# A fused two-layer graph network: the fold of two attention units one product earlier, the range check behind the keys, the last store in two halves

## The chip, the core and the metric

The kernel runs on one core of one Trainium2 chip. Five engines work side by side: TensorE (PE) multiplies matrices, with its weight loads shown as a row of their own (PEld); VectorE (DVE) and ScalarE (ACT) do elementwise work and reductions; GpSimd (POOL) does a little elementwise work; SyncE (SP) issues nearly all DMAs. The metric is the device time of one execution in microseconds (us). Three runs of the kernel before give 2157.03 to 2157.29, median 2157.13.

## What is computed

Sixteen batch elements x of 1024 nodes and 256 channels pass through two layers; adj is a 1024 by 1024 matrix, the same for all. All is in float32.

```python
# layer 0
c_adj = mean of x over channels                      # one number a node
A     = abs(abs(sigmoid(c_adj[j] - c_adj[i]) - 0.5) - 0.5) * 2
Wg    = adj * (A + A.T) / 2
g     = relu((x.T @ Wg) * para)                      # 256 x 1024
q     = g.T in 4 heads of 64;  k, v = x @ kv_w in 4 heads
out   = softmax(q @ k.T * scale) @ v
x     = layernorm(x + out)
# layer 1: two graph convolutions, 256 -> 128 -> 256
h = relu(x @ w1_loop + adj @ (x @ w1_neigh) + b1)
h = relu(h @ w2_loop + adj @ (h @ w2_neigh) + b2)
x = layernorm(x + (x + h) * 0.5)
```

## The kernel before

The kernel sets its order of work by hand: each engine runs its instructions in the order in which `run()` (from line 973, it calls all parts) writes them down. One pass of its loop treats one batch element b: attention of b, in between the graph convolutions of b - 1 and b - 2 and the last normalisation of b - 3, and then the queries, keys and values of b + 1.

**Attention.** The work of one b is cut into four units (`UNITS`: two pairs of heads by two halves of the query nodes). `scores(u)` makes eight score tiles on PE, takes their exponential on ACT (L629) and sums them on DVE over the key tiles (L633, L635); a transpose and a reduction (L637, L640) leave partial denominators in `den_part`. `outputs(u)` multiplies with the values on PE (L648) and transposes the result on DVE (L653). `add(*units)` is the fold of the change's name. A small matmul with the constant `fold` sums the partial denominators over partitions (L662). DVE takes the reciprocal (L668), and for each unit scales the output, adds it to x and takes channel sums (L672, L674, L675). After the last unit the two halves of the sums are joined (L256), and `rden_min` and `rden_max` note the extremes of the reciprocals for this b (L678, L679). These two feed nothing but the check at the very end: if a reciprocal left a given range, a slow, safe version of everything is run.

**Queries.** For b + 1 the product x.T @ Wg is made with seven block products in place of eight (`FastQueries`), on four steps k of 128 rows. `likeness` makes A on ACT, `times_adj` multiplies by adj on DVE (L496), `right` makes the sums of blocks T that the seven products need (L549 to L552, four instructions of DVE), and `pair(k)` does both for step k. `step(k)` issues the seven products on PE (L577), in the order 1, 2, 3, 5, 7, 6, 4, and in the last step 1, 6, 2, 7, 4, 5, 3. Products 5 and 6 read T. A function can be handed to a step (`halfway`); it is called ahead of product 7. The lines of `run()` that concern the change, for every b from 1 to 14:

```python
q.pair(2)
q.step(0)
q.step(1, lambda: att.add(*((2, 3) if both else (3,))))
q.pair(3)
q.step(2, norm.mean)
q.load_para()
kv.load()
q.step(3)
qT = q.end(norm.sum_squares, norm.squares)
```

So DVE's queue reads: products with adj and T of pair 2, the fold of units 2 and 3, products with adj and T of pair 3, the mean. PE's reads: steps 0 and 1 with the small matmul inside, steps 2 and 3. In the first pass of this kind (b = 1) unit 2 has been folded before, and step 1 folds unit 3 alone.

**Keys and values.** `kv.run` interleaves seven products each for keys and values on PE with copies on ACT and additions on DVE; the last addition is L461. In its midst the variance is folded, and POOL takes the power -0.5 (L328). Behind it `norm.scale` multiplies x by that (L333), and `norm.spread` transposes it (L221) and stores it by nodes (eight DMAs, L341).

**The end.** For the last b, `ending` treats the output in quarters of two node tiles. The first three are normalised on ACT, the last on DVE (`normalize`, L289), and each is stored with one DMA (L876). Behind the last store SP loads the result of the range check into a register and branches on it (L1213, L1214).

Buffers: 25 row tiles of 128 by 1024 are handed out in turn (`row_tile`), and PSUM (the memory that PE writes) has three tiles of two banks and two of one bank.

Of the kernel before, what the change touches and what calls it, by code (L numbers as in the profile page):

```python
# [18 lines left out]
def kernel(  # L19
# [266 lines left out]
    def normalize(mv, rstd, xb, count=NT):  # L286

        for t in range(count):
            nc.vector.tensor_scalar(xb[:, t, :], xb[:, t, :], mv[:, t, 0:1], rstd[:, t:t + 1],  # L289
                                    op0=ALU.subtract, op1=ALU.mult)  # L290
# [223 lines left out]
    class FastQueries(Queries):  # L514
# [42 lines left out]
            self.times_adj(TJ + k)  # L557
            self.right(k)

        def step(self, k, halfway=None):  # L560
            if k == 0:
                a, b, c = (big_psum(f"g_ps_{self.b}_{i}") for i in range(3))
                h0, h1 = ts(0, FB), ts(1, FB)
                self.p = {1: a[:, h0], 6: a[:, h1], 2: b[:, h0], 7: b[:, h1], 5: c[:, h0], 3: c[:, h1],
                          4: bank_psum(f"g_ps_{self.b}_3")}
            lo, hi = self.wg.pop(k), self.wg.pop(TJ + k)
            t12, t4 = self.T.pop(k)
            h0, h1 = ts(0, FB), ts(1, FB)
            terms = {1: (self.block(0, 0), lo[:, h0]), 2: (self.block(0, 1), hi[:, h0]), 3: (self.S[3], hi[:, h1]),
                     4: (self.block(1, 1), t4), 5: (self.S[0], t12[:, h0]), 6: (self.S[1], t12[:, h1]),  # L570
                     7: (self.S[2], lo[:, h1])}

            for n in (1, 6, 2, 7, 4, 5, 3) if k == TJ - 1 else (1, 2, 3, 5, 7, 6, 4):
                if n == 7 and halfway:
                    halfway()
                x_n, w_n = terms[n]
                nc.tensor.matmul(self.p[n], x_n[:, k, :], w_n, start=(k == 0), stop=(k == TJ - 1))  # L577
# [26 lines left out]
    class Attention:  # L604
# [50 lines left out]
        def add(self, *units):  # L655

            b, half = self.b, FB // S
            u0, n = units[0], len(units)
            pd = bank_psum(f"den_ps_{b}_{u0}")
            den = pd[:, 0:2 * half * n]  # L660
            part = [self.parts.pop(u) for u in units][0]
            nc.tensor.matmul(den, fold.rearrange("p a k -> p (a k)"),  # L662
                             part[:, u0 % 2:u0 % 2 + n, :].rearrange("p u k -> p (u k)"), start=True, stop=True)
            den = den.rearrange("p (u s h) -> p u s h", u=n, s=2)
            rden = self.rden[:, u0 * half:(u0 + n) * half].rearrange("p (u h) -> p u h", u=n)
            for s in range(2):
                rows = slice(s * HD, (s + 1) * HD)
                nc.vector.reciprocal(rden[rows], den[rows, :, s, :])  # L668
            for k, u in enumerate(units):
                pair, j = UNITS[u]  # L670
                o = by_node(self.o.pop(u))
                nc.vector.tensor_mul(o, o, rden[:, k, :].unsqueeze(2).to_broadcast([P, half, S]))  # L672
                dst = by_node(self.xB[pair][:, ts(j, FB)])
                nc.vector.tensor_add(dst, dst, o)  # L674
                nc.vector.tensor_reduce(self.sums[:, pair, ts(j, half)], dst, AX.X, ALU.add)  # L675
            if u == len(UNITS) - 1:
                join(self.sums)
                nc.vector.tensor_reduce(rden_min[:, b:b + 1], self.rden, AX.X, ALU.min)  # L678
                nc.vector.tensor_reduce(rden_max[:, b:b + 1], self.rden, AX.X, ALU.max)  # L679

    def safe_attention(b, xb, qT, kT, v):

# [54 lines left out]
    class GraphConv:  # L737
# [119 lines left out]
        def ending(self, dst, rows01, aside):  # L857

            per = FB // C
            parts, banks = [], {}

            def leave(g, mv, rstd, aside=True):
                rows = self.x[:, g * per:(g + 1) * per, :]
                if aside:
                    shift = small.tile([P, per], F32, tag="shift_e", name=f"shift_e_{g}", bufs=2)
                    nc.vector.tensor_scalar_mul(shift, mv[:, :, 0], -1.0)
                    nc.gpsimd.tensor_mul(shift, shift, rstd)  # L870
                    for i in range(per):
                        nc.scalar.activation(rows[:, i, :], rows[:, i, :], AF.Identity, bias=shift[:, i:i + 1],
                                             scale=rstd[:, i:i + 1])
                else:
                    normalize(mv, rstd, rows, per)
                nc.sync.dma_start(out=dst[g * per * P:(g + 1) * per * P, :].rearrange("(t p) c -> p t c", p=P), in_=rows)  # L876

            def bias(g):
                banks[g] = (bank_psum if g % 2 else half_psum)(f"h2e_ps_{g}")
                nc.scalar.copy(banks[g].rearrange("p (i c) -> p i c", c=C),  # L880
                               b2_sb.unsqueeze(1).to_broadcast([P, per, C]))

            def quarter(g):
                p2 = banks.pop(g)
                self.outer(g, per, p2, onto=True)
                rows = self.x[:, g * per:(g + 1) * per, :]
                nc.vector.scalar_tensor_tensor(rows, p2.rearrange("p (i c) -> p i c", c=C), 0.0, rows,
                                               op0=ALU.max, op1=ALU.add)
                mv = small.tile([P, per, 2], F32, tag="mv_e", name=f"mv_e_{g}", bufs=2)
                statistics(mv, rows, range(per), f"e{g}")  # L890
                rstd = reciprocal_deviation(mv, f"e{g}", EPS2, per)
                parts.append((g, mv, rstd))

            self.second(rows01, lambda: (bias(0), bias(1), aside(), bias(2), bias(3), quarter(0)))
            leave(*parts.pop())
            for g in range(1, NT // per):
                quarter(g)
                leave(*parts.pop(), aside=g + 1 < NT // per)
# [74 lines left out]
    def run():  # L973
# [57 lines left out]
        for b in range(B):  # L1031
# [85 lines left out]
            if more and not c1:  # L1117
                kv = KeysValues(b + 1, ready["xT"])
                for t in range(3, NT):
                    q.load(t)  # L1120
                for t in range(3, NT):
                    q.likeness(t)
                tiles[2] = adj_blocked(2)
                q.times_adj(3)
                q.step(0)
                q.times_adj(4)
                q.step(1)
                att.add(3)
                for mt in (3, 5, 6, 7):
                    tiles[mt] = adj_blocked(mt)  # L1130
                q.load_para()
                q.times_adj(5)
                q.step(2)
                q.step(3)
                norm.mean()
                q.times_adj(6)
                q.times_adj(7)
                q.step(4)
                norm.squares()
                norm.sum_squares()  # L1140
                q.step(5)
                q.step(6)
                kv.sums()
                kv.load()
                norm.variance()
                xB = load_blocked(b + 1, f"a{b + 1}")
                q.step(7)
                qT = q.end()
                load_next()
                kT, v = kv.run(later=lambda: (norm.scale(), norm.spread(), turn_adj((2, 3))))  # L1150
                turn_adj((5, 6, 7))
            elif more:
                q.pair(2)
                q.step(0)
                q.step(1, lambda: att.add(*((2, 3) if both else (3,))))
                q.pair(3)
                q.step(2, norm.mean)
                q.load_para()
# [3 lines that stand above are left out]
                xB = load_blocked(b + 1, f"a{b + 1}")  # L1162
                load_next()
                kT, v = kv.run(norm.variance, q.scale)
                if not c2:
                    adj_sums(rows01, 3)
                norm.scale()
                norm.spread()
            else:
                c2.load_h1()  # L1170
                c2.load_x()
                both.fetch(2, 3)
                c1.inner()
                both.left(nc.gpsimd)
                both.fetch(1, 4)
                both.run({1: (lambda: att.add(3),), 2: (norm.mean, norm.squares, norm.sum_squares), 7: (norm.variance,),
                          5: (norm.scale, norm.spread)})
                c1.turn(0)
                c2.last()
                c1.turn(1)  # L1180
# [86 lines left out]
```

## Time and profile before

| what | value |
|---|---|
| median of 3 runs | 2157.13 us (2157.03 to 2157.29) |
| the profiled execution | 2157.04 us, its span 2155.3 us |
| granted TensorE clock | 0.998 |
| one pass of the loop | about 132.6 us |
| DVE L668, reciprocal on 64 x 32 | 0.35 us, 52 of them |
| DVE L678, minimum over 64 columns | 0.21 us, 16 of them |
| DVE L551 and L552, one T block | 0.68 and 0.69 us |
| POOL L328, power on 128 x 32 | 6.24 us, 16 of them |
| last four stores, issue to landing | 2.1 to 4.4 us, median 3.4 |

The busy time of PE comes from matmuls whose ends are modelled, and its instructions overlap; the time from one start to the next is the surer measure. A wait is put down to the semaphore that came last. A line of the timeline reads: start, duration, engine, line, operation, out<-in, shape, count, and in brackets the idle time before it with what ended it.

### The profile page before, as it was taken

Reading aid. Unit: us, or ns where it says so; the run is one execution under the profiler, and the core shown is the slowest. Engines: PE = TensorE matmul, PEld = TensorE weight load, DVE = VectorE, ACT = ScalarE, POOL = GpSimd, SP = SyncE. Lnnn points to the kernel's source line nnn. Section 1 sums busy time; section 2 is a strip of 40 time slices with the busy share of each in tenths; the row PEclk is TensorE's granted clock in tenths of the full one; section 3 lists DMA queues with packets and bytes.
Section 4 is the critical chain, followed back from the end, with each engine's and each line's share of the span. In section 5 each row is a group of like instructions: output and inputs, shape, how many; then the busy total and the mean of one; then the engine's idle time right before and its main releaser. Section 6 shows DMA issues by size and latency. Waiting matters only on the chain.

```text
span 2155.3 us, 23725 instructions
## 1 busy us (share of the span) xinstructions
PE 2142.7 (99%) x8360; PEld 1021.6 (47%) x8360; DVE 1903.6 (88%) x2350; ACT 1042.7 (48%) x1374; POOL 358.2 (17%) x201
## 2 busy tenths in 40 slices
PE   9999999999999999999999999999999999999997
PEld 5344444544445444444544445454454444544354
DVE  5999988989999899989999898999899898999964
ACT  5745545545345454445544555445553445545412
POOL 1010130211303113030120302203021130211021
PEclk9999999999999999999999999999999999999999
DMA  9393654736557275472756637565374553734442
GB/s 237 117 147 117 148 156 112 152 108 134 144 143 173 86 132 156 132 171 88 123 167 130 157 91 119 172 127 156 110 115 156 128 156 121 133 128 95 120 138 98
DMA packets 612192, 290.73 MB, mean 135 GB/s; under 512 B 504801, under 2 KB 569697, under 8 KB 612065
## 3 DMA queue, kind: packets, MB, share of 16 engines
q1 hardware_dynamic: 611792, 288.87, 55.6%
q8 instruction: 68, 1.11, 0.2%
q14 instruction: 60, 0.48, 0.1%
q10 hardware_dynamic: 272, 0.26, 0.0%
HBM read 242.35 MB, written 46.72 MB: 134 GB/s over the span
## 4 chain that ended last, share of the span: by engine, by line


## 5 line engine op out<-in xcount | busy, mean ns | idle before, releaser
L629 ACT ACTIVATE pr<-s 128x1024 f32<-128x1024 f32 x512 | 476.1, 1054 | 175.8 <-PE s L626 175.0
L635 DVE TENSOR_TENSOR acc<-acc,pr 128x1024 f32<-128x1024 f32 x384 | 489.2, 1274 | 42.2 <-DVE acc L635 2.4
L626 PE MATMUL s<-qT,kT 64*128 64x512 f32 x2048 | 456.8, 596 | 0.0
L648 PE MATMUL av<-pr,v 128*64 128x512 f32 x2048 | 453.6, 595 | 0.0
L626 PEld LDWEIGHTS s<-qT,kT 64*128 64x128 f32 x2048 | 190.9, 186 | 237.3 <-ACT pr L629 116.0
L328 POOL TENSOR_TENSOR rstd<-rstd,neg_half 128x32 f32<-128x32 f32 x16 | 99.8, 6238 | 1118.0 <-DVE rstd L326 1118.0
L648 PEld LDWEIGHTS av<-pr,v 128*64 128x64 f32 x2048 | 141.3, 137 | 298.7 <-issue 292.2
L490 ACT ACTIVATE wg<-c_row,c_col 128x1024 f32<-128x1024 f32 x128 | 146.1, 1141 | 75.6 <-DVE accB L637 65.7
L496 DVE SCALAR_TENSOR_TENSOR wg<-wg,adj 128x1024 f32<-128x1024 f32 x128 | 149.9, 1209 | 12.2 <-ACT wg L491 11.9
L932 PE MATMUL hu_ps<-adj,R 128*128 128x512 f32 x360 | 158.0, 595 | 0.0
L491 ACT ACTIVATE wg<-wg 128x1024 f32<-128x1024 f32 x128 | 135.3, 1057 | 4.1
L577 PE MATMUL g_ps<-wg,S 128*128 128x512 f32 x224 | 116.4, 601 | 0.0
L577 PE MATMUL g_ps<-T,S 128*128 128x512 f32 x224 | 115.7, 598 | 0.0
L577 PE MATMUL g_ps<-wg,x 128*128 128x512 f32 x224 | 109.0, 599 | 0.0
L633 DVE TENSOR_TENSOR acc<-pr,pr 128x1024 f32<-128x1024 f32 x64 | 82.0, 1282 | 29.7 <-ACT pr L629 29.7
L932 PE MATMUL hu_ps<-adjT,t 128*128 128x512 f32 x240 | 105.7, 592 | 0.0
L932 PEld LDWEIGHTS hu_ps<-adj,R 128*128 128x128 f32 x360 | 67.3, 190 | 78.9 <-issue 78.2
L586 ACT COPY P<-g_ps 128x512 f32<-128x512 f32 x14 | 8.2, 585 | 178.2 <-PE g_ps L577 178.2
L637 DVE STREAM_TRANSPOSE accB<-acc 128x1024 f32<-128x1024 f32 x64 | 79.7, 1245 | 2.2
L948 ACT COPY snap<-hu_ps 128x512 f32<-128x512 f32 x15 | 8.8, 585 | 150.2 <-PE hu_ps L932 150.2
L640 DVE TENSOR_REDUCE den_part<-accB 128x32 f32<-128x1024 f32 x64 | 78.1, 1220 | 2.2
L820 PE MATMUL h_ps<-w2n_sb,uT 128*128 128x256 f32 x240 | 72.7, 385 | 0.0
(204 smaller groups left out, 3018.1 us busy)
## 6 DMA issues: line engine op xcount, KB each, us to landing
adj<-in_adj_dram SPq DMA_DIRECT2D x128, 512.0 KB, 4.8
adj<-adjT SPq DMA_DIRECT2D x120, 512.0 KB, 10.1
para<-in_L_gnn_para_dram SPq DMA_DIRECT2D x32, 512.0 KB, 4.5
xB_a<-in_x_dram SPq DMA_DIRECT2D x128, 128.0 KB, 3.9
x1d<-xB_a SPq DMA_DIRECT2D x128, 128.0 KB, 3.4
x<-x1d SPq DMA_DIRECT2D x16, 1024.0 KB, 15.5
xB<-in_x_dram SPq DMA_DIRECT2D x120, 128.0 KB, 4.5
x<-in_x_dram SPq DMA_DIRECT2D x15, 1024.0 KB, 6.9
```

The costliest lines, as they stand in the source:

```text
L328: nc.gpsimd.tensor_tensor(self.rstd, self.rstd, neg_half, ALU.pow)
L490: nc.scalar.activation(wg, self.c_row, AF.Abs, bias=self.c_col[:, t:t + 1], scale=-1.0)
L491: nc.scalar.activation(wg, wg, AF.Tanh, scale=-0.5)
L496: nc.vector.scalar_tensor_tensor(wg, wg, 1.0, self.adj.pop(t), op0=ALU.add, op1=ALU.mult)
L577: nc.tensor.matmul(self.p[n], x_n[:, k, :], w_n, start=(k == 0), stop=(k == TJ - 1))
L626: nc.tensor.matmul(ps[:, ts(s, FB)], self.kT[rows, pair, ts(mt, P)], self.qT[rows, pair, ts(j, FB)], start=True, stop=True)
L629: nc.scalar.activation(pr, ps, AF.Exp)
L633: nc.vector.tensor_add(acc, self.pr[0], pr)
L635: nc.vector.tensor_add(acc, acc, pr)
L637: nc.vector.transpose(accB, acc)
L648: nc.tensor.matmul(pav[s * HD:(s + 1) * HD, :], self.v[:, mt, pair * P + s * HD:pair * P + (s + 1) * HD], self.pr[mt][:, ts(s, FB)], start ...
L932: nc.tensor.matmul(dst, self.x[n][:, k, :], half_adj[w][:, k, :] if w else of_rows(rows, k), start=(start and k == 0), stop=(k == TJ - 1), ...
```

## The change

Three things are done. A step gets a parameter that says ahead of which product the function is called, and step 1 is given 5 in place of 7. The two reductions of the range check leave `add` and become a function `watch`, which is called where `add` was last in the first and the last batch element, and behind `kv.run` in all others. The last quarter of the output is normalised and stored tile by tile.

```diff
-        def step(self, k, halfway=None):
+        def step(self, k, halfway=None, at=7):
...
-                if n == 7 and halfway:
+                if n == at and halfway:
                     halfway()
...
             if u == len(UNITS) - 1:
                 join(self.sums)
-                nc.vector.tensor_reduce(rden_min[:, b:b + 1], self.rden, AX.X, ALU.min)
-                nc.vector.tensor_reduce(rden_max[:, b:b + 1], self.rden, AX.X, ALU.max)
+
+        def watch(self):
+            b = self.b
+            nc.vector.tensor_reduce(rden_min[:, b:b + 1], self.rden, AX.X, ALU.min)
+            nc.vector.tensor_reduce(rden_max[:, b:b + 1], self.rden, AX.X, ALU.max)
...
                     for i in range(per):
                         nc.scalar.activation(rows[:, i, :], rows[:, i, :], AF.Identity, bias=shift[:, i:i + 1],
                                              scale=rstd[:, i:i + 1])
+                    nc.sync.dma_start(out=dst[g * per * P:(g + 1) * per * P, :].rearrange("(t p) c -> p t c", p=P),
+                                      in_=rows)
                 else:
-                    normalize(mv, rstd, rows, per)
-                nc.sync.dma_start(out=dst[g * per * P:(g + 1) * per * P, :].rearrange("(t p) c -> p t c", p=P), in_=rows)
+                    for i in range(per):
+                        normalize(mv[:, i:i + 1, :], rstd[:, i:i + 1], rows[:, i:i + 1, :], 1)
+                        t = g * per + i
+                        nc.sync.dma_start(out=dst[t * P:(t + 1) * P, :], in_=rows[:, i, :])
...
                 att.add(3)
+                att.watch()
...
-                q.step(1, lambda: att.add(*((2, 3) if both else (3,))))
+                q.step(1, lambda: att.add(*((2, 3) if both else (3,))), 5)
...
                 kT, v = kv.run(norm.variance, q.scale)
+                att.watch()
...
-                both.run({1: (lambda: att.add(3),), 2: (norm.mean, norm.squares, norm.sum_squares), 7: (norm.variance,),
+                both.run({1: (lambda: att.add(3), att.watch), 2: (norm.mean, norm.squares, norm.sum_squares), 7: (norm.variance,),
```

## The prediction, made before the changed kernel was run

> **What bounds the kernel now.** I read the page first, then the windows of one pass, then the two matmul rows of a timeline, and last the VectorE (DVE) rows in front of what TensorE (PE) waits for. The chain of waits is empty in this profile, so the limit has to be found by hand.
>
> ```profile
> PE 2142.7 (99%) x8360; PEld 1021.6 (47%) x8360; DVE 1903.6 (88%) x2350; ACT 1042.7 (48%) x1374; POOL 358.2 (17%) x201
> ```
>
> PE is busy for all but 12.6 us of 2155.3. That is no proof that no time is lost, since an end of a matmul is modelled: stalls hide in it. So I look at distances. A pass over one batch element repeats; its mark is the first matmul of step 0 of the graph product (L577).
>
> ```profile
> 226.42 0.70 PE L577 MATMUL g_ps<-wg,x 128*128 128x512 f32 x1
> ...
> 358.76 0.70 PE L577 MATMUL g_ps<-wg,x 128*128 128x512 f32 x1
> ...
> 491.37 0.70 PE L577 MATMUL g_ps<-wg,x 128*128 128x512 f32 x1
> ...
> 623.97 0.70 PE L577 MATMUL g_ps<-wg,x 128*128 128x512 f32 x1
> ```
>
> The distances are 132.34, 132.61 and 132.60 us. The passes are equally full, apart from one thing: the first folds unit 3 alone in step 1, all later ones fold units 2 and 3. So something costs 0.26 us in each later pass. The weight loads of step 3 show where:
>
> ```profile
> 1039.91 0.19 PEld L577 LDWEIGHTS g_ps<-wg,x 128*128 128x128 f32 x1 [0.24 <-issue]
> 1040.34 0.19 PEld L577 LDWEIGHTS g_ps<-wg,x 128*128 128x128 f32 x1 [0.24 <-issue]
> 1041.36 0.30 PEld L577 LDWEIGHTS g_ps<-T,S 128*128 128x128 f32 x2 [0.82 <-DVE T L551]
> 1041.89 0.19 PEld L577 LDWEIGHTS g_ps<-wg,x 128*128 128x128 f32 x1 [0.24 <-issue]
> ```
>
> A matmul is two passes of 0.43 us, with a load every 0.43. The load after 1040.34 was due at 1040.77 and comes at 1041.36, 0.59 late. Four loads after 1040.34 would start the product after next at 1041.63 instead of 1041.89: 0.26 us lost, the same number as between the distances. By the starts of all matmuls this gap (product 1 to product 6 of step 3) occurs in 13 passes, 0.151 to 0.157 us at its first half and 0.105 at its second. In the first pass the load is late too (idle 0.55 at 245.73, so 0.31 over the usual 0.24), and its matmul starts at 245.85, in step: up to about 0.3 us of lateness is free.
>
> What the load waits for is T of pair 3, the last link of a DVE queue:
>
> ```profile
> 1030.04 0.69 DVE L552 TENSOR_TENSOR T<-wg,T 128x512 f32<-128x512 f32 x1
> 1031.68 0.72 DVE L668 RECIPROCAL rden<-den_ps 64x32 f32<-64x32 f32 x2 [0.95 <-PE den_ps L662]
> ...
> 1036.66 0.19 DVE L256 TENSOR_TENSOR sums<-sums 128x32 f32<-128x32 f32 x1
> 1036.77 0.21 DVE L678 TENSOR_REDUCE rden_min<-rden 128x1 f32<-128x64 f32 x1
> 1036.90 0.21 DVE L679 TENSOR_REDUCE rden_max<-rden 128x1 f32<-128x64 f32 x1
> ...
> 1040.62 0.69 DVE L551 TENSOR_TENSOR T<-wg,T 128x512 f32<-128x512 f32 x1
> ```
>
> From the reciprocal to T (ends 1041.30) DVE has no gap; ahead of the reciprocal it idles 0.95 us for the fold of the denominators on PE. Any earlier start there arrives at T in full.
>
> **What the Trainium skill says.** "Perfetto Trace Analysis", section Identifying the Most-Contended Engine, calls matmul busy time a poor measure and asks for the gaps and the semaphore behind each. The trace agrees: a window of 132.60 us over a whole pass shows PE busy for 132.60, the stall inside. "TensorE: Matmul & The Clock Gate", section LDWEIGHTS, gives columns / 1.2, an estimate of 107 ns for 128; in the pair of loads at 1041.36 (0.30 us for two of 0.19) the second starts 0.11 later. It is this unhidden load that makes the second half of the stall (0.105). "Runtime: NRT & Kernel Launch", section Instruction fetch mechanics, says that a taken branch outside the fetched window must fetch its target by DMA. In this trace SyncE (SP) spends 3.5 us between its branch and its next instruction:
>
> ```profile
> L1214 SPq EVENT_SEMAPHORE  x8: 17/17/17, 2153.3 to 2153.9; - x8
> ...
> L1214 SPq COMPARE_BRANCH  x1: 50/50/50, 2149.8 to 2149.8; - x1
> ```
>
> "DMA: Bandwidth & Descriptors", section on the anatomy of one DMA, puts a fixed part of about 2 us into every transfer. The four last stores here land 2.1 to 4.4 us after issue, so halving one saves little of it.
>
> **The change, part by part.** (1) Fold one product sooner. Step 1 runs products 1, 2, 3, 5, 7, 6, 4; the fold moves from after 5 to ahead of 5. PE issues the same instructions; the bubble of 56 ns around the small matmul (short matmul, load not hidden) moves along: 0. The fold's two loads come at 1030.03 instead of 1030.88, 0.85 us earlier. Its own inputs are early: the last is the transpose of unit 3's output (L653, 1025.13 to 1025.84), 4.2 us before. So it adds no wait, and product 5 behind it has its T since 1025. The reciprocal could then start at 1030.83; DVE ends L552 at 1030.73 and usually goes on within 0.05. Gain for the DVE queue: 0.85 us (0.80 to 0.95).
>
> (2) Range check out of the way. The two reductions hold the queue from 1036.77 to 1037.02, where the next product with the adjacency starts: 0.25 us. Together T of pair 3 is ready 1.10 us earlier, at 1040.20, and its load is due at 1040.77. The stall is gone with 0.57 us to spare, and with the free 0.3 even one part would nearly do: the fold alone leaves 0.59 - 0.85 < 0, the check alone leaves a load 0.34 late, a few hundredths over what was free. So 13 x 0.261 = 3.39 us of PE time go. In the pass without the stall nothing is gained.
>
> What is late next? Nothing on PE that I can find: product 4 needs T4, 1.1 earlier now; the sum for the mean was ready at 1036.85 for a load at 1037.12. After that DVE runs up against PE's own products at the end of step 3, so that its lead of 1.1 us melts to PE's 0.26.
>
> Where the check lands: behind the last addition of the values.
>
> ```profile
> 1059.38 0.69 DVE L461 TENSOR_TENSOR v<-vsnap,v_ps 128x512 f32<-128x512 f32 x1 [0.20 <-PE v_ps L406]
> 1060.69 2.36 DVE L333 TENSOR_TENSOR xB_a<-xB_a,rstd 128x1024 f32<-128x1024 f32 x2 [0.63 <-POOL rstd L328]
> ```
>
> DVE idles 0.63 us there for the power on GpSimd (POOL), which ends at 1060.66. The two reductions take some 0.13 + 0.21 = 0.34 us from 1060.0, so they end near 1060.3: cost 0, cover left about 0.3. Without that cover it would be 0.34 us at the head of scale, transposes and eight stores. In the pass with the adjacency sums (once) they delay these by 0.25, ahead of the same wait: 0. In the first and the last batch element the two instructions keep their place.
>
> Moving the fold also changes the order in which row buffers come free: 11 of the row tiles of a pass get another predecessor. The tightest new pair is a load of x blocks (issued at 1047.0) behind a matmul of step 2 that was over at 1038.8. That is 8 us: cost 0.
>
> (3) Last quarter by node tile. One store of 256 KB, issued at 2148.79 for 0.37 us, becomes two of 128 KB. The first can be issued when tile 0 is normalised (2148.44), to 2148.84; the second follows after the 0.04 that issues stand apart, to 2149.25 if it too takes 0.37, against 2149.16 before. SP's load of the check value and its branch stand behind them, then the 3.5 us of fetching. The old store had landed at 2152.2, 1.1 us before SP went on, so its landing isn't the end, and the halves bring nothing: +0.09 us. Bounds: 0.0 with the issue of a half at 0.33 (the short ones of this trace), and -0.4 if the landing should decide after all. I take +0.05.
>
> Sum against the profiled execution (2157.04, span 2155.3 and 1.7 around it): 2157.04 - 3.39 + 0.05 = 2153.7. The median is 0.09 above this execution: 2153.8.
>
> **Rivals.** The forecast: stall gone, 2153.8. For it: the pass with no stall runs now, and is 0.26 shorter. Range of its own 2153.3 to 2154.5.
>
> Stall stays or half stays: the wait put down to T could be another, or another DVE delay takes up the lead. For it: releasers are inferred. Against: T ends at 1041.30 and the load follows 0.06 later; the first pass, whose DVE queue is shorter, has no loss. 2155.5 for half, 2157.2 for all.
>
> Slower: the check ahead of the scale becomes a delay. Place: DVE between L461 and L333. If the power were done before about 1060.3, or the reductions took over 0.6 us beside it, scale, transpose and stores would slip by up to 0.34, and SP's queue of loads behind these stores with them. Carried through to PE in 14 passes that is 4.8 us; with the stall gone 2153.8 + 4.8 = 2158.6. It decides only where a DMA or x1T is what PE waits for. Against it: the first product on x1T starts at 1073.35, after the transposes ended at 1065.33, and waits for PE.
>
> **How the numbers follow.** Forecast 0.86, stall (partly) kept 0.07, slower rival 0.04, something unseen 0.03. The range of 2152.9 to 2155.6 takes in the forecast's bounds and the half-kept stall. A difference of 0.2%, 4.3 us, is what a measurement here can be trusted to tell from none; the expected gain of 0.155% lies under it. Faster by more needs 1 us beyond every stall that I count: 0.06. Slower by more (over 2161.4) is beyond even the slow rival: 0.03. Within: 0.91.
>
> **What would show it.** In the new trace: marks 132.34 us apart in all passes; loads of product 6 in step 3 at the 0.24 idle of all others, no long wait for L551; the reciprocal within 0.1 us of L552; L333 still released by POOL; two stores at the end 0.41 apart, and SP's first instruction after the branch again some 3.5 us after it. The prediction is wrong if the distance stays at 132.60 or if L333 is no longer released by POOL.

## The result, and the profile after

| | before | after |
|---|---|---|
| median of 22 runs each | 2157.15 us (2156.74 to 2158.65) | 2153.64 us (2153.06 to 2154.27) |
| ratio, 95% interval | | 0.9984 (0.9977 to 0.9990) |
| the profiled execution, span | 2157.04, 2155.3 | 2154.23, 2152.5 |
| first mark (step 0 of the first pass) | 226.42 | 227.40 |
| distance of the marks, pass 1 | 132.34 | 132.34 |
| distance of the marks, later passes | 132.60 | 132.34 |
| load of product 6 in step 3 late by, later passes | 0.58 | 0.00 |
| end of L289 to the end of the span | 6.50 | 6.07 |

The kernel is faster by 3.5 us, 0.16%. First the marks of the new kernel, from the timeline of PE (start, duration, engine, line, operation, names, shape):

```profile
227.40 0.70 PE L577 MATMUL g_ps<-wg,x 128*128 128x512 f32 x1
...
359.74 0.70 PE L577 MATMUL g_ps<-wg,x 128*128 128x512 f32 x1
...
492.08 0.70 PE L577 MATMUL g_ps<-wg,x 128*128 128x512 f32 x1
...
624.42 0.70 PE L577 MATMUL g_ps<-wg,x 128*128 128x512 f32 x1
```

All distances are now 132.34. The first mark, on the other hand, comes 0.98 us later than in the profile of before. That is the start of the program, which the change doesn't touch: in the twelve profiles of this study the first mark lies anywhere from 226.22 to 227.40. So the spans of two single profiles can't be set against each other to better than a microsecond; distances and medians of many runs can.

The weight loads of step 3 in the same pass as before:

```profile
1039.60 0.19 PEld L577 LDWEIGHTS g_ps<-wg,x 128*128 128x128 f32 x1 [0.24 <-issue]
1040.02 0.19 PEld L577 LDWEIGHTS g_ps<-wg,x 128*128 128x128 f32 x1 [0.24 <-issue]
1040.45 0.19 PEld L577 LDWEIGHTS g_ps<-T,S 128*128 128x128 f32 x1 [0.24 <-issue]
1040.88 0.19 PEld L577 LDWEIGHTS g_ps<-T,S 128*128 128x128 f32 x1 [0.24 <-issue]
1041.31 0.19 PEld L577 LDWEIGHTS g_ps<-wg,x 128*128 128x128 f32 x1 [0.24 <-issue]
```

A load every 0.43, the product with T as any other. And the DVE queue in front of it, with the place where the check now stands:

```profile
1029.73 0.69 DVE L552 TENSOR_TENSOR T<-wg,T 128x512 f32<-128x512 f32 x1
1030.50 0.72 DVE L668 RECIPROCAL rden<-den_ps 64x32 f32<-64x32 f32 x2
...
1035.48 0.19 DVE L256 TENSOR_TENSOR sums<-sums 128x32 f32<-128x32 f32 x1
1035.59 1.22 DVE L496 SCALAR_TENSOR_TENSOR wg<-wg,adj 128x1024 f32<-128x1024 f32 x1
...
1059.40 0.21 DVE L681 TENSOR_REDUCE rden_min<-rden 128x1 f32<-128x64 f32 x1
1059.53 0.21 DVE L682 TENSOR_REDUCE rden_max<-rden 128x1 f32<-128x64 f32 x1
1060.11 2.36 DVE L333 TENSOR_TENSOR xB_a<-xB_a,rstd 128x1024 f32<-128x1024 f32 x2 [0.37 <-POOL rstd L328]
```

The reciprocal follows T4 of pair 2 within 0.08 (L552 ends at 1030.42), where 0.95 us were idle. The check sits in the idle time ahead of the scale and leaves 0.37 of it; POOL still releases the scale.

### The profile page after: what moved, and what is told of

Read it like the earlier page. It is cut to its first block, busy times and chain, and to the rows that moved or that the text cites. A ratio compares the mean times of both kernels' runs of the same rounds, so it can differ in the third digit from the quotient of the medians.

```text
span 2152.5 us, 23740 instructions
## 1 busy us (share of the span) xinstructions
PE 2138.9 (99%) x8360; PEld 1023.1 (48%) x8360; DVE 1905.3 (89%) x2350; ACT 1039.9 (48%) x1374; POOL 361.1 (17%) x201
## 4 chain that ended last, share of the span: by engine, by line
```

## The experiments

All times are medians, with the distance of the marks in the passes after the first, and the lateness of the load, from each one's profile. "Against before" is the difference to the kernel before in the same comparison. Fold alone, check alone, halves alone and fold with check were timed together; so were the four kernels with repeated checks or ACT's help, and the last two; the change stands by itself. Each group has its own runs of the kernel before, whose medians went from 2156.92 to 2157.15. Most intervals reach some 1.4 us to either side, so a gain of 3 us is clear in the times, and 0.2 us between two kernels is not.

| kernel | us (runs) | against before | ratio (95% interval) | distance | product 6 late by |
|---|---|---|---|---|---|
| the change | 2153.64 (22) | -3.51 | 0.9984 (0.9977 to 0.9990) | 132.34 | 0.00 |
| fold alone | 2153.87 (21) | -3.22 | 0.9985 (0.9978 to 0.9991) | 132.34 | 0.00 |
| check moved alone | 2153.86 (21) | -3.23 | 0.9985 (0.9978 to 0.9991) | 132.35 | 0.33 |
| halves alone | 2157.05 (13) | -0.04 | 1.0000 (0.9992 to 1.0008) | 132.60 | 0.58 |
| fold and check, one store | 2153.90 (21) | -3.19 | 0.9985 (0.9979 to 0.9992) | 132.34 | 0.00 |
| fold, check four times at its old place | 2157.20 (13) | +0.12 | 1.0001 (0.9993 to 1.0009) | 132.51 | 0.49 |
| fold, check seven times at its old place | 2168.35 (5) | +11.27 | 1.0053 (1.0039 to 1.0067) | 133.27 | 1.25 |
| the change, check five times behind the keys | 2153.62 (21) | -3.46 | 0.9984 (0.9978 to 0.9991) | 132.34 | 0.00 |
| the change, first half stored by ACT | 2153.71 (21) | -3.37 | 0.9984 (0.9977 to 0.9991) | 132.34 | 0.00 |
| the change, fold ahead of product 3 | 2153.51 (21) | -3.41 | 0.9984 (0.9978 to 0.9991) | 132.34 | 0.00 |
| the change, both stores written behind both halves | 2153.51 (21) | -3.41 | 0.9984 (0.9977 to 0.9990) | 132.34 | 0.00 |

### One part at a time

The fold alone:

```diff
-q.step(1, lambda: att.add(*((2, 3) if both else (3,))))
+q.step(1, lambda: att.add(*((2, 3) if both else (3,))), 5)
```

> The fold ahead of product 5, all else as before. Theory (T of pair 3 comes 0.59 us late on DVE, about 0.33 of lateness is free): DVE gains 0.85 us, the stall goes in all 13 passes, distance of the marks 132.34, time 2153.7. Rival A (the parts add up, each pays for its own 0.25 or 0.85 in proportion): about 2154.5. Rival B (the wait isn't DVE's): 2157.1.

It does all that the change does for PE: 132.34, 2153.87. Its load of product 6 comes in step:

```profile
1038.99 0.19 PEld L577 LDWEIGHTS g_ps<-wg,x 128*128 128x128 f32 x1 [0.24 <-issue]
1039.42 0.19 PEld L577 LDWEIGHTS g_ps<-T,S 128*128 128x128 f32 x1 [0.24 <-issue]
```

The check alone, `watch` called where the change calls it, fold and store as before:

```diff
-                nc.vector.tensor_reduce(rden_min[:, b:b + 1], self.rden, AX.X, ALU.min)
-                nc.vector.tensor_reduce(rden_max[:, b:b + 1], self.rden, AX.X, ALU.max)
...
                 kT, v = kv.run(norm.variance, q.scale)
+                att.watch()
```

> The range check behind the keys, all else as before: DVE's lead is 0.25 us only, the load of product 6 is 0.34 late. Theory: as 0.33 is free, nearly the whole stall goes all the same, loss left 0.00 to 0.05 a pass, distance 132.34 to 132.39, time 2153.7 to 2154.4. Rival A (in proportion, 0.25 of 1.10): gain 0.8, 2156.3. Rival C (the fold's place on PE is what stalls): no gain, 2157.1.

This one tells the theories apart, since it moves DVE by 0.25 us only. Loads of PE in its profile:

```profile
1040.01 0.19 PEld L577 LDWEIGHTS g_ps<-wg,x 128*128 128x128 f32 x1 [0.24 <-issue]
1040.77 0.30 PEld L577 LDWEIGHTS g_ps<-T,S 128*128 128x128 f32 x2 [0.57 <-DVE T L551]
1041.31 0.19 PEld L577 LDWEIGHTS g_ps<-wg,x 128*128 128x128 f32 x1 [0.24 <-issue]
```

The load still waits for T, 0.57 us of idle time where the kernel before has 0.82. Yet the distance of the marks is 132.35: 0.01 us lost, against 0.26. The matmuls of the same stretch show why:

```profile
1040.01 1.02 PE L577 MATMUL g_ps<-wg,x 128*128 128x512 f32 x2
1040.87 1.03 PE L577 MATMUL g_ps<-T,S 128*128 128x512 f32 x2
1041.73 0.59 PE L577 MATMUL g_ps<-wg,x 128*128 128x512 f32 x1
```

A load in step starts a whole pass, some 0.43 us, ahead of its matmul (1041.31 and 1041.73). The late load of product 6 is only 0.10 ahead (1040.77 and 1040.87), and its matmul is in step all the same, two passes or 0.86 after that of product 1. A product has two loads, though. The second of a late product starts 0.11 behind the first, and in all twelve profiles its own matmul follows 0.43 behind it, never less. So it is the second load that sets the loss: nothing is lost as long as the lateness and 0.11 together stay under 0.43, that is up to 0.32. Why the lead of the first load can be used up and that of the second cannot is not shown. The wait is real in both kernels; only what exceeds 0.32 of lateness costs. An idle time in front of a row of this trace is thus no measure of what its removal brings.

Halves alone:

```diff
-                    normalize(mv, rstd, rows, per)
+                    for i in range(per):
+                        normalize(mv[:, i:i + 1, :], rstd[:, i:i + 1], rows[:, i:i + 1, :], 1)
+                        t = g * per + i
+                        nc.sync.dma_start(out=dst[t * P:(t + 1) * P, :], in_=rows[:, i, :])
```

> The last quarter stored in two halves, all else as before. Theory of the prediction: +0.05, 2157.2; SP's branch sets the end, not the landing. Rival D (the one profiled execution of the changed kernel, whose end behind the last normalisation is 0.43 shorter, is typical): 2156.7.

2157.05 against the 2157.09 of the kernel before says no change, but with 13 runs from 2156.4 to 2159.8 it can't tell 0.05 from -0.4. And the counterpart, fold and check with one store:

> The changed kernel with its last quarter stored by one DMA, as before. Theory: 2153.7, the same as with the halves to 0.1. Rival D (the halves are worth 0.4): 2154.1.

2153.90, against 2153.64 with halves in another comparison. It lies between the two expectations, so neither experiment excludes that the halves are worth 0.4. The end is taken up below.

### The size of the stall

Here the fold stays ahead of product 5, and the check stays at its old place but is repeated, to push T of pair 3 back in known steps:

```diff
+                for _ in range(4):
-                nc.vector.tensor_reduce(rden_min[:, b:b + 1], self.rden, AX.X, ALU.min)
-                nc.vector.tensor_reduce(rden_max[:, b:b + 1], self.rden, AX.X, ALU.max)
+                    nc.vector.tensor_reduce(rden_min[:, b:b + 1], self.rden, AX.X, ALU.min)
+                    nc.vector.tensor_reduce(rden_max[:, b:b + 1], self.rden, AX.X, ALU.max)
```

> Fold ahead of product 5, the range check at its old place but made four times (three extra pairs, 0.25 us each): DVE's lead falls from 0.85 to 0.10, the load is 0.49 late. Theory: 0.16 us lost a pass in 13 passes, distance 132.50, time 2153.7 + 2.1 = 2155.8. Rival C (the fold's place on PE decides): 2153.7.

> The same with the check made seven times (six extra pairs, 1.5 us): DVE is 0.65 us behind the kernel before, the load is 1.24 late. Theory: 0.91 us lost in 13 passes and 0.63 in the first, distance 133.25, time 2153.7 + 12.5 = 2166.2. Rival C: 2153.7. Rival A (in proportion to the lead, from 0.26 lost at 0 to none at 1.10): about 0.4 a pass, 2159.

The second kernel has 7 in place of 4. The loads of product 6, first with four checks, then with seven:

```profile
1041.42 0.19 PEld L577 LDWEIGHTS g_ps<-wg,x 128*128 128x128 f32 x1 [0.24 <-issue]
1042.34 0.30 PEld L577 LDWEIGHTS g_ps<-T,S 128*128 128x128 f32 x2 [0.72 <-DVE T L551]
```

```profile
1045.82 0.19 PEld L577 LDWEIGHTS g_ps<-wg,x 128*128 128x128 f32 x1 [0.24 <-issue]
1047.50 0.30 PEld L577 LDWEIGHTS g_ps<-T,S 128*128 128x128 f32 x2 [1.49 <-DVE T L551]
```

Lateness is the distance of the two starts less 0.43: 0.49 and 1.25. With 0.32 free that makes losses of 0.17 and 0.93; the distances say 132.51 - 132.34 = 0.17 and 133.27 - 132.34 = 0.93. So the whole curve is there: 0.33 late costs 0.01, 0.49 costs 0.17, 0.58 costs 0.26, 1.25 costs 0.93. From 0.32 on every hundredth counts in full. The rivals that saw it in proportion to DVE's lead, or in the fold's place on PE, are out: the fold stands at the same place in both kernels.

Both times are nevertheless higher than expected, 2157.2 for 2155.8 and 2168.35 for 2166.2. Most of the difference lies in the first pass. Its load in the kernel with four checks:

```profile
247.30 0.30 PEld L577 LDWEIGHTS g_ps<-T,S 128*128 128x128 f32 x2 [1.68 <-DVE T L551]
```

It is 1.44 late, where I had reckoned with 0.31 - 0.85 + 0.75 = 0.21; the first distance is 133.46, 1.12 over the others' floor. Two things were left out. The fold brings the first pass nothing, since DVE doesn't wait there: before the change its reciprocal starts at 238.32 and L552 ends at 238.40, and with the fold alone that load is still 0.32 late. And the repeated check also stands in the batch element ahead (b = 0), whose delay reaches over: DVE's first L549 behind the first mark starts 0.92 us after it in the kernel before and in the changed one, but 1.27 to 1.28 after it in the three kernels that repeat the check at b = 0. With five checks behind the keys, where only b = 0 has its checks in the old spot, the first load is 0.43 late instead of 0.05 to 0.07. Together 0.32 + 0.75 + 0.36 = 1.43, against 1.44 measured. With seven checks the first load is 2.20 late and the first distance 134.22, which is 1.25 over what was expected of it. Why the share of b = 0 is 0.36 whether the check is made four, five or seven times isn't shown. Of the errors of the two times, 0.3 and 0.9 us (the latter from five runs) lie outside the first pass and weren't traced further.

### The slower rival

The check five times behind the keys:

```diff
         def watch(self):
             b = self.b
+            for _ in range(5):
...
```

> The changed kernel with the range check behind the keys made five times, some 1.4 us where the cover is 0.63: the scale is 0.7 us late. Theory: transposes end 8 us before PE asks for them, so nothing is lost: 2153.7, distance 132.34. Rival (slower rival of the prediction, the delay runs through stores and loads to PE): 0.7 x 14 = 9.8, 2163.5.

The last two of the ten reductions and what follows, from DVE's timeline:

```profile
1059.74 0.21 DVE L682 TENSOR_REDUCE rden_min<-rden 128x1 f32<-128x64 f32 x1
1059.87 0.21 DVE L683 TENSOR_REDUCE rden_max<-rden 128x1 f32<-128x64 f32 x1
1060.00 2.35 DVE L333 TENSOR_TENSOR xB_a<-xB_a,rstd 128x1024 f32<-128x1024 f32 x2
1062.27 2.37 DVE L221 STREAM_TRANSPOSE x1T<-xB_a 128x1024 f32<-128x1024 f32 x2
```

No bracket: the scale has no idle time before it and no longer waits for POOL. From the start of L461 it comes after 1.88 us (1058.12 to 1060.00), in the changed kernel after 1.31 (1058.80 to 1060.11), so it is 0.57 late. And PE, at the product that reads the transposes:

```profile
1072.10 1.08 PEld L756 LDWEIGHTS t_ps<-w1n_sb,x1T 128*128 128x128 f32 x9 [0.81 <-PE av L648]
```

It waits for PE's own previous product, as ever. The time is 2153.62. So the cover isn't needed: even with it gone, the slack behind it takes the delay, since the transposes end at 1064.64, 7.5 us before PE loads them.

### More lead than is needed

```diff
-q.step(1, lambda: att.add(*((2, 3) if both else (3,))), 5)
+q.step(1, lambda: att.add(*((2, 3) if both else (3,))), 3)
```

> The changed kernel with the fold ahead of product 3, another 0.86 us sooner. Theory: no stall is left and the reciprocal already follows T4 of pair 2 within 0.08, so it can't start sooner; distance 132.34, time 2153.6. Rival A (DVE's lead is worth something of itself): below 2153.3.

2153.51, or -3.41 against before: nothing further. The reciprocal starts at 1029.79, while L552 has its last tenth of a microsecond to go; DVE is the limit there now, and PE needs no more.

### The end

First the changed kernel with ACT issuing the first half:

```diff
-nc.sync.dma_start(out=dst[t * P:(t + 1) * P, :], in_=rows[:, i, :])
+(nc.sync if i else nc.scalar).dma_start(out=dst[t * P:(t + 1) * P, :], in_=rows[:, i, :])
```

> The changed kernel, the first half of the last store issued by ACT instead of SP. In its profile SP's second issue takes 0.75 us behind the first, where single issues take 0.37. Theory (SP's issue, load of the check value and branch set the end): SP is free 0.4 us sooner, 2153.2 to 2153.3. Rival D' (landing of the store or ACT's own branch sets the end): 2153.6 or more.

It gave 2153.71, no gain on the 2153.64. Then both stores behind both normalisations:

> The changed kernel, but both halves of the last store issued behind the second normalisation, so the first no longer starts 0.3 us sooner; SP is free later. If the 0.25 between kernels with halves (2153.62 to 2153.64) and with one store (2153.86 to 2153.90) comes from the start of the first half: 2153.9 or more. If it comes from the smaller last store: 2153.6 to 2153.7. If it is noise: anything between.

```diff
+                    normalize(mv, rstd, rows, per)
                     for i in range(per):
-                        normalize(mv[:, i:i + 1, :], rstd[:, i:i + 1], rows[:, i:i + 1, :], 1)
```

But a store waits for its own tile alone, and the first was issued at 2145.35, ahead of the end of the second normalisation at 2145.65. So the order on the chip was that of the changed kernel, and the run answers nothing but how well a time repeats: -3.41 where the change has -3.51.

SP's instructions at the branch, for the changed kernel (L1223), then for the one with a single store (L1219), then with the first half issued by ACT (L1223):

```profile
L1223 SPq EVENT_SEMAPHORE  x8: 17/17/17, 2150.5 to 2151.1; - x8
...
L1223 SPq COMPARE_BRANCH  x1: 50/50/50, 2147.8 to 2147.8; - x1
```

```profile
L1219 SPq EVENT_SEMAPHORE  x8: 17/17/17, 2149.8 to 2150.4; - x8
...
L1219 SPq COMPARE_BRANCH  x1: 50/50/50, 2146.2 to 2146.2; - x1
```

```profile
L1223 SPq EVENT_SEMAPHORE  x8: 17/17/17, 2149.7 to 2150.3; - x8
...
L1223 SPq COMPARE_BRANCH  x1: 50/50/50, 2146.5 to 2146.5; - x1
```

Set from the end of L289 (2146.38, 2145.20, 2145.43), the branch ends after 1.51, 1.05 and 1.10 us, and the next instruction comes after 4.16, 4.64 and 4.31. The later branch has the sooner end. The six profiles with one store need 6.30 to 6.63 us from L289 to the end of the span, the five with SP's two halves 5.92 to 6.12, so there this stretch is shorter by 0.2 at least and 0.46 in the mean. In time, the four kernels with fold, check and SP's halves stand at -3.41 to -3.51, and those with one store at -3.19 to -3.23 (of the latter the check alone keeps 0.12 of the stall). So the halves seem to bring some 0.2 us. The profiles show a shorter end; the size in time isn't shown, since no comparison holds both groups, and alone the halves gave 0.04.

What shortens the wait behind the branch stays open: it isn't SP's being free sooner, since with ACT's help SP is 0.4 us sooner at its branch than in the changed kernel and the time is no better. The DMA packets of the traces give a hint. Behind L289 the packets of a single store run on 16 DMA engines at a time from 1.0 to 1.6 us, and the first packet of an instruction queue (q14, 8 KB a packet) after they have begun starts at 1.52 to 1.68. With SP's halves the packets of the first are mostly over at 1.1, and that packet of q14 starts at 1.20 to 1.25. In all eleven profiles SP's next instruction comes 2.8 to 3.1 us after it, and with ACT's help, where it starts at 1.59, after 2.7. This would fit a fetch that waits for the store's packets, but no run tests it.

## Why the prediction was right, and where it was off

The forecast was 2153.8, the result 2153.64.

**The stall on T of pair 3** is shown. Distances 132.34 in all passes, the load in step, no other wait in its place, as the steps said. 13 x 0.261 = 3.39 us was read from distances in the kernel before, and all 13 are gone.

**What the parts are worth.** The prediction said that the fold alone would do and the check alone nearly. Both hold: 0.00 and 0.01 us left a pass. Their effects don't add, so of the two either could have been left out for 0.1 us.

**The free lateness of about 0.3 us** was read from one load of the first pass. The experiments make it 0.32, with full cost behind it, and trace it to the second load of the product.

**The check's new place**: cost 0, the cover left foreseen as about 0.3 and measured as 0.37. The cover holds, but the slower rival is refuted more firmly than that: with the scale 0.57 late its deciding point (PE waiting for x1T) is still 7.5 us off, as the prediction's own argument against it said.

**Row buffers in another order**: nothing shows on PE, where it would have to. It wasn't tried apart.

**The end** is the step that was off. The term of the sum was +0.05; it is about -0.2 by the times and -0.46 by the mean of the profiles. "Then the 3.5 us of fetching" took this stretch for a constant behind the branch; it is 3.3 to 3.7 with one store, and 2.5 to 3.0 with halves. The issue of the second half was taken as 0.37 us and takes 0.75 in the changed kernel, so SP was even later than expected. By the times the error is 0.25 us and inside the bounds, but the sign was wrong. That the wait behind the branch is one for fetching was taken over as settled; the runs show its length and not its cause.

**The sum.** With one store the two other parts bring 3.2 us, the distances 3.4. The last 0.2 stays unexplained; it is no more than the medians of the kernel before differ by between the comparisons (2156.92 to 2157.15). That the forecast hit within 0.2 is partly luck: this and the end make up for each other.

## What to carry to other kernels

On an engine that looks fully busy, compare the distance of marks from pass to pass; a pass with one step less, as the first here, is a free experiment that shows a stall and its size. A wait in front of a pipelined row may cost less than it lasts (here the first 0.32 us of lateness were free), so ask how late an instruction may be before asking how late it is. And of several small edits aimed at one wait, the first that is enough takes the whole gain.

## What had not been expected of the hardware

A weight load 0.33 us late cost 0.01 us, and one 0.58 late 0.26: the first of a product's two loads could be late by 0.32 for nothing. Two stores of 128 KB at the end of the program gave a shorter end in the profiles than one of 256 KB (5.9 to 6.1 us against 6.3 to 6.6 behind the last normalisation), although SP's second issue took 0.42 to 0.75 us in place of 0.37 and its branch came later. And the start of the program, up to the first mark, differs by as much as 1.2 us between profiles of kernels with the same beginning.
